# Two residual graph layers in Strassen form on one core: order of GpSimd's, VectorE's and ScalarE's side work

## The chip, the cores and the metric

The kernel runs on one core of a Trainium2 chip. The metric is the device time of one execution in microseconds (us), the median of several executions. Engines are named as in the profile: PE is TensorE's matmul, PEld its weight load, DVE is VectorE, ACT is ScalarE, POOL is GpSimd, and SP issues the DMAs.

## The reference

There are 64 graphs of 256 nodes with 512 features, in float32. Two layers run one after the other, each with a residual and a layer norm:

```
# layer 0
deg = sum(adj, -1);  agg = (adj @ x) / max(deg, 1e-6)
x1  = layernorm(x + relu(concat([x, agg]) @ W.T))
# layer 1
q, k, v = x1 @ Wqk (two halves), x1 @ Wv
w   = sum(q * (adj @ (k * mask)), -1) * mask / sqrt(512)
out = layernorm(x1 + softmax(w over the nodes) * v)
```

The softmax runs over the 256 nodes of a graph, so each node ends with one weight for its row of v. Layer norm takes mean and variance over the 512 features.

## The kernel before

**Tiling.** The graphs go in 32 pairs (`for j in range(NP)`). Every product of layer 0 is done once with W's two halves (W0), and in layer 1 with Wv and with Wq times Wk transposed (W1), which the kernel works out at its start. Each product is in Strassen form with seven products instead of eight, P1 to P7, of sums of blocks: S1 to S4 are sums of the left side, T1 to T4 of the right side. Some of the seven are split once more in the same form (`inner`). The sums of the left sides, X for layer 0 and Y for layer 1, live in a `Side`: xT_s and x1T_s in the profile, their inner sums in xT_i and x1T_i. S4 has no room of its own: in xT_s it is written over S1, in x1T_s over S2.

**Units.** A product is a list of units, each of one to three matmuls and the copies and additions that belong to it. `run("i k i k", ...)` pops units by letter, and this is TensorE's order, written out by hand. In layer 0: i is P1, k is P5, m is P2, p is P6 (left side S2), q is P7 (S3), r is P3 (left side S4), s is P4. P1 and P2 use the same bank, `pw[0]`. `inner` has four units; its third unit fills a part of the output bank by a copy on ScalarE, and the fourth accumulates onto it. l is P3 of layer 1 (`open1`), spread over the start of the next pair.

**Gather.** The products with adj are units a to g (`gather`), also seven. For layer 0, `a` and `b` end with two additions each on VectorE into own (`onto`, scalar_tensor_tensor with 1/deg), out of banks u and p2; `d`, `e` and `g` accumulate onto u. The right side is the y of layer 0, whose sums T1 to T4 (`sums_T`, tile tv) are made on VectorE. `spare()` in a, b and d pops a sum that was kept for later (`later`, `T_late`).

**Side work.** The layer norms, the masks, the degrees, the softmax and the weight sums are chains of steps. `tick`, at the end of each unit, places steps while the engine's modelled time `eng.free` isn't over `room` (0.6) ahead of the modelled clock and the chain's `ready` time is reached; lines 131 to 133 hold the modelled costs. `flush(names)` places at once whatever is left of a chain. Since every engine works in the order of the program, a step that is placed early blocks what stands behind it:

```
ready[0] = eng.free + (0.4 if eng is not vec else 2.2 if name == "finish"
                       else 0.7 if len(steps) == NT else 1.4)
```

`norm_of` is the layer norm's chain: mean (`less`, VectorE), two squares with a sum (junk, ScalarE), factor (rstd, two small ScalarE operations), `shift` (VectorE), two scales (ScalarE). "norm" is the first layer's, "finish" the second's; finish's scales release the store of out. Behind that store, on the same queue, stands the load of the next adj, and its landing starts adj's four sums on GpSimd (sa). The masked adj has four such sums too.

**The last pair** has its own code behind the loop: softmax over a row in PSUM, `b3` adds P3 and its fifth inner product on VectorE, then for each half of the rows product, `bn_stats`, factor, scale and store.

Of the kernel before, what the change touches and what calls it, by code (L numbers as in the profile page):

```python
# [35 lines left out]
F32 = mybir.dt.float32  # L36
BF16 = mybir.dt.bfloat16
AF = mybir.ActivationFunctionType
OP = mybir.AluOpType
AX = mybir.AxisListType  # L40

P = 128
# [5 lines left out]
S1, S2, S3, S4 = range(4)  # L48
# [46 lines left out]
def resnorm_kernel(  # L95
# [46 lines left out]
    def step(chain):  # L142
        _, name, ready, steps = chain
        eng, work = steps.popleft()
        work()
        ready[0] = eng.free + (0.4 if eng is not vec else 2.2 if name == "finish" else 0.7 if len(steps) == NT else 1.4) if steps and steps[0][0] is not eng else 0.0
        if not steps:
            chains.remove(chain)

# [9 lines left out]
    def flush(*names):  # L159
        while True:  # L160
            c = next((c for c in chains if not names or c[1] in names), None)
            if not c:
                return
            step(c)

    def run(order, **units):
        for name in order.split():
            units[name].pop(0)()
# [7 lines left out]
    def first(out, in_):  # L176

        return tc.keep_in_program_order(nc.sync.dma_start(out, in_))
# [101 lines left out]
                (eng, lambda: eng.tensor_sub(a(S2), a(S1), a(A11))),  # L280
                (eng, lambda: eng.tensor_sub(a(S3), a(A11), a(A21)))]

    def fourth_sums(X):

        ks = slice(0, 2)
        gp.tensor_sub(X.block(S4, ks), X.block(A12, ks), X.block(S2, ks))
        inner_sums(X, gp, 2)

    def run_now(steps):
        for _, work in steps:  # L290
            work()

    def inner_sums(X, eng, part):

        if X.s is None:
            X.open_sums()
        of_sum = lambda n: lambda k, e: X.s[:, k, X.slot[n]:X.slot[n] + 1, e]
        ks, b = ((slice(0, 2), X.first_row), (slice(2, 3), of_sum(S1)), (slice(0, 1), of_sum(S4)))[part]
        a11, a12, a21, a22 = (b(k, e) for k in range(2) for e in range(2))
        i = [X.i[:, r, ks] for r in range(4)]  # L300
        for to, op, c, d in ((i[0], OP.add, a21, a22), (i[1], OP.subtract, i[0], a11),
                             (i[2], OP.subtract, a11, a21), (i[3], OP.subtract, a12, i[1])):
            eng.tensor_tensor(to, c, d, op=op)

    def adj_sums(j):
        a, s = adjs[j], pool.tile([P, 4, 2, P], F32, name="sa", bufs=2)
        a11, a21, a12, a22 = (a[:, :, t, h * P:(h + 1) * P] for t in range(2) for h in range(2))
        gp.tensor_add(s[:, 0], a21, a22)
        gp.tensor_sub(s[:, 1], s[:, 0], a11)
        gp.tensor_sub(s[:, 2], a11, a21)  # L310
        gp.tensor_sub(s[:, 3], a12, s[:, 1])
        return {"A11": a11, "A12": a12, "A22": a22, "S1": s[:, 0], "S2": s[:, 1], "S3": s[:, 2], "S4": s[:, 3]}
# [71 lines left out]
            return go  # L384
        return [unit(e) for e in range(H)]

    def sums_T(val, later=None):

        b11, b12, b21, b22 = (val[:, :, t, h * HF:(h + 1) * HF] for t in range(NT) for h in range(2))
        tv = pool.tile([P, 4, 2, HF], F32, name="tv")  # L390
        t1, t2, t3, t4 = (tv[:, r] for r in range(4))
        vec.tensor_sub(t1, b12, b11)
        rest = [lambda args=args: vec.tensor_sub(*args) for args in ((t2, b22, t1), (t3, b22, b12), (t4, b21, t2))]
        if later is None:
            for do in rest:
                do()
        else:
            later.extend(rest)
        return {"B11": b11, "B21": b21, "B22": b22, "T1": t1, "T2": t2, "T3": t3, "T4": t4}

    def gather(a, w, dst, u, p5, p2, own=None, rdeg=None, later=()):
# [69 lines left out]
        return dict(a=[u1], b=[g2], c=[g5], d=[u2], e=[u3], f=[g3], g=[u4])  # L471


    def norm_of(src, total):

        rstd, shift, less, var = (small.tile([P, NT], F32, name=x) for x in ("rstd", "shift", "less", "var"))

        def mean():
            vec.tensor_scalar(less, total, -1.0 / F, None, op0=OP.mult)

        def square(t):
            junk = small.tile([P, F], BF16, name="junk", bufs=1)
            act.activation(junk, src[:, t], AF.Square, bias=less[:, t:t + 1], accum_out=var[:, t:t + 1])

        def factor():
            act.activation(rstd, var, AF.Ln, bias=eps, scale=1.0 / F)
            act.activation(rstd, rstd, AF.Exp, scale=-0.5)

        def shifts():
            vec.tensor_tensor(shift, less, rstd, op=OP.mult)  # L490

        def scale(t):
            act.activation(src[:, t], src[:, t], AF.Identity, bias=shift[:, t:t + 1], scale=rstd[:, t:t + 1])
        return [(vec, mean)] + [(act, lambda t=t: square(t)) for t in range(NT)] + [(act, factor), (vec, shifts)] + [
            (act, lambda t=t: scale(t)) for t in range(NT)]

    def layer_norm(src, mv, n, by_vec):

# [255 lines left out]
    for j in range(NP):  # L754
# [17 lines left out]
        if j == 0:  # L772
            run("i k i k i k i k", i=i, k=k)
            flush("degrees")
            load_rows(1)
        elif j == 1:
            early.append(a1)
            run("k i k i k i k", i=early[0], k=k)
            fourth_sums(X)
            run("m p p m p p m", m=m, p=p)  # L780
            load_x(1)
        else:
            run("i k", i=i, k=k)
            send_scores(j - 2)
            run("i l k", i=i, k=k, l=open1)
            flush("norm")
            fetch_scores(j - 2)
            places[0](range(16))
            run("i k i k", i=i, k=k)
        if j != 1:  # L790
            fourth_sums(X)
        if j > 1:
            flush("mask")
            sumsM[j - 1] = adj_sums(j - 1)
# [4 lines left out]
            softmax(j - 2)  # L799
            shared[0] = 1.0  # L800
        if j != 1:
            run("m p p m p p m", m=m, p=p)
        flush("w0a")
        run("q q q", q=q)
        flush("w0")
        run("r q r m", m=m, q=q, r=r)
        if j == 1:
            flush("norm", "mask")
            sumsM[0] = adj_sums(0)
            load_rows(2)  # L810
        quiet[0] = j < 2
        room[vec] = -9.0 if j > 1 else 0.6
        run("r s r", r=r, s=s)
# [3 lines left out]
            inner_sums(Y, gp, 0)  # L817
            queue(1, "sums", *outer_sums(Y, vec), (vec, lambda Y=Y: inner_sums(Y, gp, 1)))
        T_late = []
        T = sums_T(ys[j], T_late if j < 2 else None)  # L820

        if j == 0:
            degrees(1)
# [11 lines left out]
        if j == 0:  # L835
            sums_next()
            held = [c for c in chains if c[1] == "w1"]
            chains[:] = [c for c in chains if c[1] != "w1"]
            early.append(inner("P1", Xs[1], W0, pw[0], u, lambda fifth: early[1](fifth)))
            run("s s a b s d c e i g f", s=s, i=early[0], **g)  # L840
            quiet[0] = False
        else:
            u2, o2, y2 = o, pf, y
            b1, b2, b3, b4, b5, b6, b7, b8 = layer1(j - 1, ys[j][:, :, 0], o2, u2, y2)
            jj = inner("P1", Y, W1, pw[0], u2)
            k = inner("P2", Y, W1, y[0], o2, b2)
            if j == 1:
                turn_here(Y, owns[0], 0, pw)
                run("s", s=s)
                turn_here(Y, owns[0], 1, pw)  # L850
                inner_sums(Y, gp, 0)
                sums_Y = (*outer_sums(Y, vec), (vec, lambda: inner_sums(Y, gp, 1)))
                run("s b a s d c", s=s, **g)
                quiet[0] = False
                flush("w1")
                run("e j g f", j=jj, **g)
                queue(1, "sums", *sums_Y)
                run("k j k j k j", j=jj, k=k)
                b1(None)
                run("k", k=k)  # L860
            else:
                run("s s j s a b", s=s, j=jj, k=k, **g)
                room[vec] = 0.6
                run("j", j=jj)
                if j < NP - 1:
                    degrees(j + 1)
                run("c d j k e j", s=s, j=jj, k=k, **g)
                quiet[0] = True
                run("k", k=k)
                quiet[0] = False  # L870
                b1(None)
                run("g f", **g)
# [78 lines left out]
    for _, turn, exps in last:  # L951
        turn()
        exps()
    run("r", r=r)
    flush()
    probs[j] = small.tile([P, 2, NT], F32, name="probs", bufs=2)
    for k in range(2):
        last[k][0](pw[k])
    b3(held[0])
    for k in range(2):  # L960
        vec.tensor_copy(probs[j][:, k], pw[k][:, :NT])
    norms = []

    def close(k, t, scale):
        for _, work in scale:
            work()
        first(out[2 * j + k, t * P:(t + 1) * P], x1[:, k, t])
    for t in (1, 0):
        for k in range(2):
            o = x1[:, k, t:t + 1]  # L970
            vec.scalar_tensor_tensor(o[:, 0], vs[j][k][:, t], probs[j][:, k, t:t + 1], o[:, 0],
                                     op0=OP.mult, op1=OP.add)
            stats, scale = layer_norm(o, small.tile([P, 1, 2], F32, name="mv"), 1, (t, k) == (0, 1))
            run_now(stats + scale[:1])
            norms.append((k, t, scale[1:]))
            if len(norms) == 2:
                close(*norms.pop(0))
    close(*norms.pop(0))


# [24 lines left out]
```

## Time and profile before

| | |
|---|---|
| median of 3 executions | 1886.93 us (1886.43 to 1887.25) |
| profiled span | 1884.5 us, granted TensorE clock 0.997 |
| from the last matmul's end to the end of the span | about 13 us |
| S4 over xT_s on GpSimd | one operation, 128x512, 1.27 us |
| stage of one pair | about 57 us |

A line of the timeline gives the start and the length in us, the engine, the line of the helper that issued it (all side work is L90, all products are L173), the operation, the tiles written and read, their shapes, and how many like operations are merged. In square brackets stands idle time before it and who ended it, as the semaphores suggest.

### The profile page before, as it was taken

To read this page: it belongs to the slowest core of one execution; us is meant where nothing else is said; L and a number is where in the kernel's file an instruction comes from. 1 tells how busy PE (TensorE), PEld (TensorE's weight loads), DVE (VectorE), ACT (ScalarE), POOL (GpSimd) and SP (SyncE) were. 2 spreads that over 40 slices of the span, in tenths; PEclk is the share of its full clock that TensorE was granted. 3 is DMA by queue.
4 is the path that set the end of the run, shared out by engine and by line. 5 is a ranking of instruction groups with operands and counts; after the bars stand their busy time and mean duration, and the time that the engine had idled before them with its cause. 6 is when DMAs were issued, how large, how long until landed. Compare 5 with 4: busy or idle time off the path is not lost.

```text
span 1884.5 us, 24896 instructions
## 1 busy us (share of the span) xinstructions
PE 1861.3 (99%) x6996; PEld 1312.9 (70%) x6996; DVE 1541.9 (82%) x3182; ACT 1303.6 (69%) x3270; POOL 896.5 (48%) x1187
## 2 busy tenths in 40 slices
PE   9999999999999999999999999999999999999997
PEld 5667767767777677677677677676776777776764
DVE  7787888788888878887888888788878888878887
ACT  3667776677776677766777776777676777667765
POOL 4455453555454554435554435454445544355532
PEclk9999999999999999999999999999999999999998
DMA  6133334333333333343433343333434233433321
GB/s 225 56 74 81 99 90 118 85 97 92 103 96 103 100 83 97 90 118 85 104 88 101 96 114 89 84 98 95 112 85 108 84 102 95 118 85 88 98 62 51
DMA packets 380713, 181.26 MB, mean 96 GB/s; under 512 B 263712, under 2 KB 345248, under 8 KB 380576
## 3 DMA queue, kind: packets, MB, share of 16 engines
q1 hardware_dynamic: 380576, 179.67, 35.5%
q8 instruction: 57, 0.93, 0.2%
q14 instruction: 80, 0.66, 0.1%
HBM read 114.10 MB, written 34.06 MB: 79 GB/s over the span
## 4 chain that ended last, share of the span: by engine, by line
PE 92%; DVE 5%; ACT 1%; POOL 1%; issue 1%; DMA 0%; DVEq 0%; ACTq 0%
PE bank L173 92%; DVE own L90 2%; DVE tv L90 1%; DVE y L90 1%; POOL xT_s L90 1%; ACT y L90 0%; ACT own L90 0%; DMA wqk<-wqk_t 0%; PE bank L625 0%; ACT bank L90 0%; DVE st L90 0%; DVE t L90 0%; DVE x L90 0%; DVE v L90 0%; ACT junk L90 0%
## 5 line engine op out<-in xcount | busy, mean ns | idle before, releaser
L90 ACT COPY bank<-bank 128x256 f32<-128x256 f32 (+1 forms) x768 | 332.6, 436 | 241.0 <-PE bank L173 231.9
L90 DVE TENSOR_TENSOR y<-bank,y 128x512 f32<-128x512 f32 x256 | 170.6, 687 | 133.2 <-ACT y L90 132.2
L90 ACT ACTIVATE junk<-own,less 128x512 bf16<-128x512 f32 x252 | 182.5, 724 | 64.8 <-DVE less L90 63.9
L90 ACT ACTIVATE own<-own,shift,rstd 128x512 f32<-128x512 f32 x255 | 200.4, 812 | 0.0
L173 PE MATMUL bank<-tv,sa 128*128 128x256 f32 x768 | 194.7, 381 | 4.0 <-DVE tv L90 1.8
L90 POOL TENSOR_TENSOR x1T_s<-x1T,x1T_s 128x512 f32<-128x512 f32 x32 | 53.2, 1663 | 280.9 <-PE bank L173 280.9
L173 PEld LDWEIGHTS bank<-tv,sa 128*128 128x128 f32 x768 | 144.8, 190 | 56.0 <-issue 22.9
L90 ACT COPY y<-bank 128x512 f32<-128x512 f32 x192 | 108.9, 584 | 94.9 <-PE bank L173 93.5
L90 POOL TENSOR_TENSOR sa<-adj 128x256 f32<-128x256 f32 x128 | 95.6, 747 | 159.3 <-DMA adj<-adj_t 150.5
L173 PE MATMUL bank<-w,x1T_s 128*128 128x512 f32 (+1 forms) x384 | 168.4, 521 | 0.0
L90 POOL TENSOR_TENSOR x1T_i<-x1T 128x256 f32<-128x256 f32 x64 | 55.6, 868 | 228.6 <-DMA x1T<-turn 213.3
L173 PE MATMUL bank<-t,xT_s 128*128 128x512 f32 (+1 forms) x384 | 160.2, 526 | 2.4 <-POOL xT_s L90 1.5
L90 POOL TENSOR_TENSOR x1T_i<-x1T_s 128x128 f32<-128x128 f32 x128 | 76.6, 598 | 177.4 <-DVE x1T_s L90 174.9
L90 DVE TENSOR_TENSOR v<-bank,v 128x512 f32<-128x512 f32 x186 | 119.2, 683 | 48.8 <-PE bank L173 48.8
L173 PE MATMUL bank<-t,x1T_s 128*128 128x512 f32 (+1 forms) x384 | 158.2, 522 | 0.3 <-ACT y L90 0.3
L173 PE MATMUL bank<-w,xT_s 128*128 128x512 f32 (+1 forms) x384 | 153.2, 521 | 0.0
L173 PE MATMUL bank<-t_i,xT_i 128*128 128x256 f32 x512 | 152.7, 380 | 0.4 <-POOL sa L90 0.2
L173 PE MATMUL bank<-t_i,x1T_i 128*128 128x256 f32 x512 | 152.3, 379 | 0.1
L173 PEld LDWEIGHTS bank<-t_i,x1T_i 128*128 128x128 f32 x512 | 97.2, 190 | 67.0 <-issue 49.7
L90 ACT COPY own<-bank 128x512 f32<-128x512 f32 x128 | 71.8, 587 | 93.5 <-PE bank L173 49.4
L173 PEld LDWEIGHTS bank<-t_i,xT_i 128*128 128x128 f32 x512 | 94.9, 190 | 58.1 <-issue 46.3
L173 PE MATMUL bank<-t,x1T 128*128 128x512 f32 x256 | 130.5, 593 | 0.0
(156 smaller groups left out, 4610.1 us busy)
## 6 DMA issues: line engine op xcount, KB each, us to landing
x<-x SPq DMA_DIRECT2D x64, 512.0 KB, 5.7
xT<-x_t SPq DMA_DIRECT2D x62, 512.0 KB, 5.5
out<-own SPq DMA_DIRECT2D x62, 512.0 KB, 3.2
x1T<-turn SPq DMA_DIRECT2D x480, 64.0 KB, 2.3
adj<-adj_t SPq DMA_DIRECT2D x64, 256.0 KB, 3.8
turn<-adj SPq DMA_DIRECT2D x64, 256.0 KB, 3.0
row<-d SPq DMA_DIRECT2D x31, 256.0 KB, 4.7
wqk<-wqk_t SPq DMA_DIRECT2D x4, 512.0 KB, 5.3
```

Source lines behind the costliest of these rows:

```text
L90: return self.tc.keep_in_program_order(getattr(self.engine, name)(out, *args, **kwargs))
L173: tc.keep_in_program_order(nc.tensor.matmul(ps, a, b, start=start, stop=True, skip_group_check=True))
```

## The change

Five edits, none of which changes what is computed.

- **S4 graph by graph**: `fourth_sums` writes S4 for graph 1 and for graph 0 in two operations. In layer 0 the second comes after the first two units of P6, and the inner sums after it.
- **Later sums of y**: of the four sums of y, two (from pair 2 on) are kept for `spare()` and so stand behind the additions of a and b.
- **norm's squares later**: the chain "norm" waits 2.2 instead of 1.4 of modelled time between the mean and the squares.
- **Last variances on ScalarE**: in the last pair the first two row halves take their variance from the sum and ScalarE's squares; P3's fifth product is added by matmuls with the identity; the additions of P3 are spread.
- **First pairs' orders mixed**: in pair 0 two more units change place; in pair 1 P2's first unit comes between P1 and P5, a is ahead of b, and the flush of the masks and the masked sums move behind the first transposes.

The diff, cut to its core:

```diff
-        ready[0] = ... (0.4 if eng is not vec else 2.2 if name == "finish" else 0.7 if len(steps) == NT else 1.4) ...
+        ready[0] = ... (0.4 if eng is not vec else 0.7 if name == "norm" and len(steps) == NT else 2.2 if name in ("finish", "norm") else 1.4) ...
...
-    def fourth_sums(X):
-        ks = slice(0, 2)
-        gp.tensor_sub(X.block(S4, ks), X.block(A12, ks), X.block(S2, ks))
-        inner_sums(X, gp, 2)
+    def fourth_sums(X, ks=(1, 0)):
+        for k in ks:
+            k = slice(k, k + 1)
+            gp.tensor_sub(X.block(S4, k), X.block(A12, k), X.block(S2, k))
+        if ks[-1] == 0:
+            inner_sums(X, gp, 2)
...
-    def sums_T(val, later=None):
+    def sums_T(val, later=None, n=3):
...
+        for do in rest[:n]:
+            do()
+        if n < len(rest):
+            later.extend(rest[n:])
...
-            run("k i k i k i k", i=early[0], k=k)
-            fourth_sums(X)
-            run("m p p m p p m", m=m, p=p)
+            run("k i k m k i k", i=early[0], k=k, m=m)
+            fourth_sums(X, [1])
+            run("p p", p=p)
+            fourth_sums(X, [0])
+            run("m p p m", m=m, p=p)
...
-            fourth_sums(X)
+            fourth_sums(X, [1])
...
-            run("m p p m p p m", m=m, p=p)
+            run("m p p", m=m, p=p)
+            fourth_sums(X, [0])
+            run("m p p m", m=m, p=p)
...
-            flush("norm", "mask")
-            sumsM[0] = adj_sums(0)
-            load_rows(2)
+            flush("norm")
...
-        T = sums_T(ys[j], T_late if j < 2 else None)
+        T = sums_T(ys[j], T_late, 0 if j < 2 else 1)
...
-            run("s s a b s d c e i g f", s=s, i=early[0], **g)
+            run("s s a b s c d i e i g f", s=s, i=early[0], **g)
...
                 turn_here(Y, owns[0], 0, pw)
+                flush("mask")
+                sumsM[0] = adj_sums(0)
+                load_rows(2)
...
-                run("s b a s d c", s=s, **g)
+                run("s a b s d c", s=s, **g)
...
     run("r", r=r)
+    for k in range(2):
+        mm(y[k][:, HF:], ident, held[0])
     flush()
...
-    b3(held[0])
+    add_p3(0)
...
-    for t in (1, 0):
-        for k in range(2):
-            o = x1[:, k, t:t + 1]
-            vec.scalar_tensor_tensor(o[:, 0], vs[j][k][:, t], probs[j][:, k, t:t + 1], o[:, 0],
-                                     op0=OP.mult, op1=OP.add)
-            stats, scale = layer_norm(o, small.tile([P, 1, 2], F32, name="mv"), 1, (t, k) == (0, 1))
-            run_now(stats + scale[:1])
-            norms.append((k, t, scale[1:]))
-            if len(norms) == 2:
-                close(*norms.pop(0))
-    close(*norms.pop(0))
+    for k in range(2):
+        total = small.tile([P, 1], F32, name="total2", bufs=2)
+        stt(k, 1, accum_out=total)
+        steps = norm_of(x1[:, k, 1:2], total, 1)
+        run_now(steps[:3])
+        norms.append((k, 1, steps[3:]))
+    add_p3(1)
+    for k in range(2):
+        stt(k, 0)
+        stats, scale = layer_norm(x1[:, k, 0:1], small.tile([P, 1, 2], F32, name="mv"), 1, k == 1)
+        run_now(stats)
+        close(*norms.pop(0))
+        run_now(scale[:1])
+        norms.append((k, 0, scale[1:]))
+    for norm in norms:
+        close(*norm)
```

More of the change, by code (lines that the diff above doesn't have):

```diff
@@ L145, in step @@
         work()
-        ready[0] = eng.free + (0.4 if eng is not vec else 2.2 if name == "finish" else 0.7 if len(steps) == NT else 1.4) if steps and steps[0][0] is not eng else 0.0
+        ready[0] = eng.free + (0.4 if eng is not vec else 0.7 if name == "norm" and len(steps) == NT else 2.2 if name in ("finish", "norm") else 1.4) if steps and steps[0][0] is not eng else 0.0
         if not steps:
@@ L393, in sums_T @@
         rest = [lambda args=args: vec.tensor_sub(*args) for args in ((t2, b22, t1), (t3, b22, b12), (t4, b21, t2))]
[L394 to L398, printed above, removed]
+        for do in rest[:n]:
+            do()
+        if n < len(rest):
+            later.extend(rest[n:])
         return {"B11": b11, "B21": b21, "B22": b22, "T1": t1, "T2": t2, "T3": t3, "T4": t4}
@@ L471, in gather, with norm_of @@
         return dict(a=[u1], b=[g2], c=[g5], d=[u2], e=[u3], f=[g3], g=[u4])
-    def norm_of(src, total):
-        rstd, shift, less, var = (small.tile([P, NT], F32, name=x) for x in ("rstd", "shift", "less", "var"))
+    def norm_of(src, total, n=NT):
+        rstd, shift, less, var = (small.tile([P, n], F32, name=x) for x in ("rstd", "shift", "less", "var"))
         def mean():
@@ L493, in scale @@
             act.activation(src[:, t], src[:, t], AF.Identity, bias=shift[:, t:t + 1], scale=rstd[:, t:t + 1])
-        return [(vec, mean)] + [(act, lambda t=t: square(t)) for t in range(NT)] + [(act, factor), (vec, shifts)] + [
-            (act, lambda t=t: scale(t)) for t in range(NT)]
+        return [(vec, mean)] + [(act, lambda t=t: square(t)) for t in range(n)] + [(act, factor), (vec, shifts)] + [
+            (act, lambda t=t: scale(t)) for t in range(n)]
     def layer_norm(src, mv, n, by_vec):
@@ L958, in resnorm_kernel, with add_p3, stt, close @@
         last[k][0](pw[k])
-    b3(held[0])
+    def add_p3(k):
+        vec.tensor_add(vs[j][k][:, 0], y[k], vs[j][k][:, 0])
+    def stt(k, t, **more):
+        vec.scalar_tensor_tensor(x1[:, k, t], vs[j][k][:, t], probs[j][:, k, t:t + 1], x1[:, k, t],
+                                 op0=OP.mult, op1=OP.add, **more)
+    def close(k, t, scale):
+        run_now(scale)
+        first(out[2 * j + k, t * P:(t + 1) * P], x1[:, k, t])
+    add_p3(0)
     for k in range(2):
@@ L962, in resnorm_kernel @@
     norms = []
[L964 to L967, printed above, removed]
-    for t in (1, 0):
-        for k in range(2):
-            o = x1[:, k, t:t + 1]
-            vec.scalar_tensor_tensor(o[:, 0], vs[j][k][:, t], probs[j][:, k, t:t + 1], o[:, 0],
-                                     op0=OP.mult, op1=OP.add)
-            stats, scale = layer_norm(o, small.tile([P, 1, 2], F32, name="mv"), 1, (t, k) == (0, 1))
-            run_now(stats + scale[:1])
-            norms.append((k, t, scale[1:]))
-            if len(norms) == 2:
-                close(*norms.pop(0))
-    close(*norms.pop(0))
+    for k in range(2):
[14 more added lines that the diff above has]
+        close(*norm)
 def kernel(x, adj, nodemask, L0_gnn_W, L1_gnn_Wqk, L1_gnn_Wv):
```

## The prediction

> **What bounds the kernel now.** I read the busy times first, then the starts of successive matmuls (how much later than the plain spacing of 0.43 us for 512 columns and 0.215 for 256 does each begin?), then the timeline round the late ones.
>
> ```profile
> PE 1861.3 (99%) x6996; PEld 1312.9 (70%) x6996; DVE 1541.9 (82%) x3182; ACT 1303.6 (69%) x3270; POOL 896.5 (48%) x1187
> ```
>
> TensorE is the bound, at a granted clock of 0.997; the change removes no matmul and adds two. So it can only move late starts and the two ends. Late starts of over 60 ns sum to 28.6 us: 9.7 before 95 us (pairs 0 and 1), 16.6 in the steady pairs, 2.4 after 1835 us; behind them lies a tail of 13.5 us. The steady 16.6 are three kinds: 7.2 us where unit p starts (22 pairs; 5.5 of waiting and 0.075 each for the restart), 3.4 us in nine pairs where gather's d follows c, and 5.9 us at P5's third unit, which the change leaves alone.
>
> Gather's d, pair 22:
>
> ```profile
> 1285.60 1.26 DVE L90 TENSOR_TENSOR y<-y,fifth 128x512 f32<-128x512 f32 x1
> 1286.89 1.10 DVE L90 TENSOR_TENSOR tv<-y 128x512 f32<-128x512 f32 x1
> 1288.02 0.69 DVE L90 TENSOR_TENSOR tv<-y,tv 128x512 f32<-128x512 f32 x1
> 1288.63 0.68 DVE L90 TENSOR_TENSOR tv<-y 128x512 f32<-128x512 f32 x1
> 1289.23 0.68 DVE L90 TENSOR_TENSOR tv<-y,tv 128x512 f32<-128x512 f32 x1
> 1289.60 2.29 PE L173 MATMUL bank<-tv,sa 128*128 128x256 f32 x8
> 1289.83 1.65 DVE L90 SCALAR_TENSOR_TENSOR own<-bank,rdeg,own 128x256 f32<-128x256 f32 x4
> ```
>
> The eight tv,sa matmuls are c and d; four should take 0.86 us, but d begins at 1290.76, 0.30 late. It writes bank u, which the first two of the four additions must read first; those stand behind four sums T1 to T4 of y.
>
> Unit p, pair 18:
>
> ```profile
> 1036.42 0.72 POOL L90 TENSOR_TENSOR sa<-adj,sa 128x256 f32<-128x256 f32 x1
> ...
> 1036.62 0.81 DVE L90 TENSOR_TENSOR v<-v,fifth 128x256 f32<-128x256 f32 x1
> ...
> 1038.40 1.30 DVE L90 STREAM_TRANSPOSE turn<-own 128x512 f32<-128x512 f32 x2
> 1039.52 1.27 POOL L90 TENSOR_TENSOR xT_s<-xT,xT_s 128x512 f32<-128x512 f32 x1 [2.37 <-PE bank L173]
> 1039.62 1.39 DVE L90 TENSOR_TENSOR bank<-bank,fifth 128x256 f32<-128x256 f32 x4
> ...
> 1040.06 1.07 ACT L90 COPY own<-bank 128x512 f32<-128x512 f32 x2 [1.45 <-DVE bank L90]
> ...
> 1040.79 1.96 PE L173 MATMUL bank<-t,xT_s 128*128 128x512 f32 x4
> ```
>
> The list of waits names POOL's S4 (xT_s, ending 1040.79). That is not the releaser: in pairs with no stall p starts 0.22 us before S4 ends, and in every late pair it starts 0.14 us after ScalarE's first copy of own ends. That copy waits for VectorE, which lost time at v<-v,fifth: 0.43 alone, 0.81 here, beside GpSimd's last sa operation.
>
> [...]v<-v,fifth (both inputs in SBUF) takes 0.43 to 1.01 us, while bank<-bank,fifth beside S4 keeps its 0.40. [...]I count sa by its starts, 0.69 to 0.80 apart.
>
> **Part by part.**
>
> *Later sums of y (n=1).* T1 and T2 stay ahead, T3 and T4 move behind the additions of a and b. The additions then follow T2: 1288.63 instead of 1289.83, 1.2 us earlier, and d is 0.3 late. The next user of T3 is e, behind c, d, j and k, over 3 us on; T4 is needed by g. Gone: nine late starts of 0.19 to 0.30 and their restarts of 0.105, **-3.4 us**. At pairs 0 and 1 all three sums were already deferred.
>
> *S4 by graph.* Two half operations (0.73 each, as the 256-element sa) for one of 1.27. In steady pairs GpSimd now does S4 of graph 1, the four masked sa (2.9 us), then S4 of graph 0 and four inner sums (2.6 with the first): it starts 1.05 us before p and ends 5.1 us after it; P3, the first reader, comes 7.3 us after p. Nothing waits, and the wait it seems aimed at is ScalarE's: **0**.
>
> *norm's squares later (2.2 for 1.4).* In steady pairs ScalarE stood idle 1.51 us for `less` (to 1133.62, in pair 19). Following `step` and `tick` with their own costs: graph 0's squares come one and three units later, graph 1's factor falls behind gather's copy of g, and the two last finish scales run behind both. From g's copy at 1142.05: 0.47 + 0.42 + 0.72 + 0.82 ends them at 1144.48 instead of 1144.26, **0.2 us** later. They release the store of out, and the load of adj is queued behind that store; its landing starts the four sa beside v<-v,fifth. Set against when p is due, the first sa begins 6.38 to 6.11 us before it in 18 late pairs (0.17 to 0.44 late, rising one for one), 6.08 to 5.86 before in eight on-time pairs (9.56 in pair 2), and 5.81, 5.76 and 5.34 before in three that are 0.06, 0.11 and 0.34 late: a sawtooth[...]. Shifting all of them by 0.2 us and reading the sawtooth again leaves 5.4 of the 7.2 us, **-1.8 us**; by 0.3 it leaves 3.9, by 0.5 it makes 7.9. Next behind the finish scales is P3's first copy (due 1144.59): 0.1 us of room.
>
> *First pairs.* Pair 0: c before d, and P1's second unit moved up to the wait of g: 0.43 us of work inside stalls, -0.4. Pair 1: m's first unit uses the bank of P1 (pw[0]) and waits for i's last copies, +0.4. More: by the same bookkeeping norm's last residual now stands ahead of P1's fifth additions on VectorE, which went at 58.17; they go at 58.9, own is copied at 59.4, and p starts near 60.1 instead of 59.36: +0.75 with all before it. Then the flush of norm:
>
> ```profile
> 69.89 0.15 DVE L90 TENSOR_TENSOR shift<-less,rstd 128x2 f32<-128x2 f32 x1
> ...
> 70.62 1.28 DVE L90 TENSOR_TENSOR own<-bank,own 128x512 f32<-128x512 f32 x2
> 70.66 1.51 ACT L90 ACTIVATE own<-own,shift,rstd 128x512 f32<-128x512 f32 x2
> ...
> 72.07 0.58 ACT L90 COPY bank<-bank 128x512 f32<-128x512 f32 x1
> ...
> 72.70 0.70 PE L173 MATMUL bank<-t_i,xT_s 128*128 128x256 f32 x2 [0.67 <-ACT bank L90]
> ```
>
> Now the shift precedes P2's additions to own (1.28, then 0.98 with fifth). With the factor one unit later, the shift isn't ready when P2 ends and is flushed behind them: additions from about 71.3, shift near 73.4, two scales 1.5, P3's copy 0.57, P3's last unit near 75.7 instead of 72.70: +3.0, the 0.75 included, although the wait before P3's third unit (0.4) goes. Afterwards a ahead of b lets d wait less (1.3 before; now some 0.3 at a and 0.3 to 0.5 at d): -0.5. Together **+2.5 us** (1.0 to 3.3). The masks' flush finds nothing left, so the masked sums moved behind it cost nothing.
>
> *The end.* Fifth is added by two identity matmuls (0.86 us) instead of two DVE additions (0.34 of spacing each); one of P3's two additions moves behind the first products; two bn_stats and bn_aggr (0.81 a graph) become squares on ScalarE, which waits there anyway. Before, the first product began at 1872.90. Now: PE ends 1869.99 + 0.86 = 1870.85, the eight small matmuls 1.05, copies to 1872.15. Then VectorE: two times 0.81 (product, mean), addition 0.62, two times 1.65 (product 0.79, stats 0.73, the rest): ready at 1877.7. ScalarE: scale 0.72, factor 0.5, last shift 0.2 and scale 0.55: about 1879.9, against 1880.82: **-0.9 us** (0.5 to 1.2). The store after it is the same.
>
> Sum: -3.4 - 1.8 + 2.5 - 0.9 = -3.6: 1886.9 - 3.6 = **1883.3**.
>
> **Rivals.** (A) The sum above, 1883.3. (B) The adj loads shift 0.3 us, where most sawtooth waits vanish (-3.3), and the second pair costs only 1.0, because VectorE's backlog is shorter than I carried over: -3.4 - 3.3 - 0.9 + 1.0 = -6.6, 1880.3. For it: 18 of 29 pairs lie just before the quiet stretch. Against: g's copy fixes the shift near 0.2. (C) The loads stay or go 0.4 later (no gain, waits of 0.2 to 0.4 in most pairs) and the second pair costs 3.3: -3.4 - 0.9 + 3.3 = -1.0, 1885.9. For it: the waits depend on landings that vary by 0.5 us. (D) Slower: the finish scales slip further, P3's first copy is late, and its second unit stalls 0.3 + 0.075 us in 29 pairs: +10.9 - 3.4 - 0.9 + 2.5 = +9.1, 1896.0. For it: 0.1 us of room at the copy and 0.17 in the bank. Against: the chain from g's copy is counted from steps that the trace times.
>
> **How the numbers follow.** A 0.40, B 0.33, C 0.20, D 0.07. The bound for faster is 1886.93 less 0.2%, 1883.2; A lies on it and counts 0.19 to faster, 0.21 to same. Faster 0.19 + 0.33 = 0.52; same 0.21 + 0.20 = 0.41; slower 0.07. The range takes in B with another 1.3 us[...] (1879.0) and C with 0.9 for the early pairs (1886.8), and leaves out D.
>
> **What would show it.** Right: no late d in steady pairs; `less` idle of ScalarE down from 1.5 us; p still late in part of the pairs, by other amounts, always 0.14 us after ScalarE's copy; P3's last unit of pair 1 over 2 us later than 72.70; the span ending about 11.7 us after the last small matmul (13.2 before). Wrong: p never late (then S4 or the loads were worth 7 us), new late starts at P3's second unit, or pair 1 finishing as early as before.

## The result, and the profile after

The changed kernel takes 1885.65 us (median of 4 runs, 1884.56 to 1886.5) against 1887.09 (4 runs, 1886.43 to 1887.43) for the kernel before, beside it on the chip: ratio 0.9992, 95% interval 0.9975 to 1.001. That is -1.4 us and can't be told from no change. The forecast, 1883.3, was 2.4 us too low. The profiled spans are 1884.5 before and 1883.9 after.

The busy line of the page, and from the list of waits of TensorE its three largest (in total, times, longest, us), both of the changed kernel:

```profile
PE 1860.9 (99%) x7000; PEld 1314.8 (70%) x7000; DVE 1511.7 (80%) x3180; ACT 1309.5 (70%) x3274; POOL 909.7 (48%) x1251
```

```profile
PE bank L173 <- ACT bank L90: 4.4, 3, 3.6
PE bank L173 <- POOL sa L90: 1.9, 8, 0.3
PE bank L173 <- ACT own L90: 1.3, 1, 1.3
```

TensorE is still the bound. New is one wait of 3.6 us for ScalarE. I measured all stages in one way: a late start is the start of a matmul less the start of the one before, less the plain spacing. Places in the first pairs are measured from the first xT_i product, which itself begins at a different time in every run:

| us | before | after | difference |
|---|---|---|---|
| first xT_i product of pair 0, from the span's start | 20.14 | 21.44 | +1.30 |
| p of pair 1, from that product | 39.21 | 39.96 | +0.75 |
| first transposes of pair 1 | 53.53 | 57.01 | +3.48 |
| first x1T_s product of pair 1 | 72.37 | 76.69 | +4.32 |
| late starts of p, steady pairs | 7.18 | 5.36 | -1.83 |
| late starts of d, steady pairs | 3.46 | 0.00 | -3.46 |
| last softmax's transposes to the last operation | 12.19 | 11.22 | -0.97 |

The first and the last four rows add up to -0.64; the two spans differ by -0.61. So these places account for the whole difference between the two traces. Each column is one execution, though, and the start and the waits of p differ from one execution to the next.

**The cost: pair 1.** The timeline where P3's last unit (t_i,xT_s into bank) is due, changed kernel:

```profile
72.71 1.28 DVE L90 TENSOR_TENSOR own<-bank,own 128x512 f32<-128x512 f32 x2
...
74.03 0.70 DVE L90 TENSOR_TENSOR own<-own,fifth 128x512 f32<-128x512 f32 x1
74.65 0.67 DVE L90 TENSOR_TENSOR shift<-less,rstd 128x2 f32<-128x2 f32 x1
...
75.36 1.52 ACT L90 ACTIVATE own<-own,shift,rstd 128x512 f32<-128x512 f32 x2 [2.83 <-DVE shift L90]
...
76.78 0.57 ACT L90 COPY bank<-bank 128x512 f32<-128x512 f32 x1
...
77.41 0.70 PE L173 MATMUL bank<-t_i,xT_s 128*128 128x256 f32 x2 [3.63 <-ACT bank L90]
...
78.45 1.91 PE L626 MATMUL bank<-ident,own 128*128 128x128 f32 x8
...
80.16 1.80 PE L173 MATMUL bank<-t,agg 128*128 128x512 f32 x2
...
81.79 1.04 PE L626 MATMUL bank<-ident,own 128*128 128x128 f32 x8
```

Read it upward from the matmul at 77.41. It waited 3.63 us for a copy of ScalarE; the copy stood behind two scales, the scales waited 2.83 us for the shift, and the shift stood behind VectorE's additions. Before, the shift came ahead of the additions, at 69.89. Now look at the lengths below it: eight transposes took 1.91 us at 78.45 and 1.04 at 81.79, and the two t,agg matmuls 1.80, where before they took 1.02. The windows view of the same trace says why. After the stretch and its length stand the busy times of PE, PEld, DVE, ACT and POOL with their instructions, then the granted clock of TensorE, the DMA share and GB/s:

```profile
60.00:77.00 17.00, 12.52 (x39) 7.05 (x38) 13.40 (x29) 12.97 (x31) 6.87 (x10) 1.00 0.46 155
77.00:82.00 5.00, 4.59 (x16) 3.29 (x17) 2.67 (x4) 1.84 (x5) 0.00 (x0) 0.66 0.00 0
```

Asked in shorter stretches, the same view gives a clock of 1.00 from 77.41 to 78.30, 0.50 from 78.30 to 81.70 and 1.00 behind that. So TensorE ran at half speed for 3.4 us (transposes 0.213 us apart, not 0.109), which costs half of that, 1.7 us. The drop came 0.9 us after work had begun again (77.41 to 78.30).

**The gain: d.** Pair 22 again, changed kernel:

```profile
1288.61 0.69 DVE L90 TENSOR_TENSOR tv<-y,tv 128x512 f32<-128x512 f32 x1
1289.22 0.87 DVE L90 SCALAR_TENSOR_TENSOR own<-bank,rdeg,own 128x256 f32<-128x256 f32 x2
...
1290.01 0.68 DVE L90 TENSOR_TENSOR tv<-y 128x512 f32<-128x512 f32 x1
1290.20 1.89 PE L173 MATMUL bank<-tv,sa 128*128 128x256 f32 x8
1290.60 0.87 DVE L90 SCALAR_TENSOR_TENSOR own<-bank,rdeg,own 128x256 f32<-128x256 f32 x2
1291.39 0.68 DVE L90 TENSOR_TENSOR tv<-y,tv 128x512 f32<-128x512 f32 x1
```

The additions of a stand straight behind T2, T3 and T4 follow them, and the eight matmuls of c and d run through in 1.89 us (2.29 before).

**Half a gain: p.** One of the pairs still late, changed kernel:

```profile
1553.85 0.73 POOL L90 TENSOR_TENSOR sa<-adj,sa 128x256 f32<-128x256 f32 x1
1553.86 1.00 DVE L90 TENSOR_TENSOR v<-v,fifth 128x256 f32<-128x256 f32 x1
...
1556.76 0.73 POOL L90 TENSOR_TENSOR xT_s<-xT,xT_s 128x256 f32<-128x256 f32 x1 [2.18 <-PE bank L173]
1557.06 1.39 DVE L90 TENSOR_TENSOR bank<-bank,fifth 128x256 f32<-128x256 f32 x4
...
1557.49 1.07 ACT L90 COPY own<-bank 128x512 f32<-128x512 f32 x2 [1.64 <-DVE bank L90]
...
1558.22 1.96 PE L173 MATMUL bank<-t,xT_s 128*128 128x512 f32 x4 [0.25 <-POOL sa L90]
```

S4 of graph 1 (xT_s) now ends at 1557.49, 0.7 us ahead of p, and p is late all the same; "POOL sa" in the bracket can't be the releaser either, since p reads no sa. The chain is the one of before: sa beside v<-v,fifth (1.00 instead of 0.43), the additions, ScalarE's first copy of own, and p 0.14 us after that copy. Late by over 60 ns are now 15 pairs instead of 20. (The 22 pairs of the prediction are those whose second matmul shows the restart; of these there are now 17.)

**The end.** The last softmax's transposes begin at 1868.63 before and at 1868.99 after, so I count from them. The first product begins 3.48 us behind them (forecast: 1872.15, that is 3.52; before: 4.27), and the last operation ends 11.22 us behind them (forecast: 1879.9, that is 11.3; before: 12.19).

### The profile page after: what moved, and what is told of

Its sections match the earlier page's. It is cut to its first block, busy times and chain, and to the rows that moved or that the text cites. A ratio compares the mean times of both kernels' runs of the same rounds, so it can differ in the third digit from the quotient of the medians.

```text
span 1883.9 us, 25002 instructions
## 1 busy us (share of the span) xinstructions
PE 1860.9 (99%) x7000; PEld 1314.8 (70%) x7000; DVE 1511.7 (80%) x3180; ACT 1309.5 (70%) x3274; POOL 909.7 (48%) x1251
## 4 chain that ended last, share of the span: by engine, by line
PE 96%; POOL 1%; issue 1%; DVE 1%; ACT 0%; DMA 0%; DVEq 0%; POOLq 0%; ACTq 0%
PE bank L173 96%; POOL xT_s L90 1%; POOL xT_i L90 0%; DVE own L90 0%; POOL sa L90 0%; DMA wqk<-wqk_t 0%; PE bank L626 0%; ACT own L90 0%; ACT bank L90 0%; DVE st L90 0%; ACT y L90 0%; PE bank L649 0%; DVE tv L90 0%; DVE shift L90 0%; DVE bank L90 0%
## 5 line engine op out<-in xcount | busy, mean ns | idle before, releaser
L90 POOL TENSOR_TENSOR x1T_s<-x1T,x1T_s 128x256 f32<-128x256 f32 x64 | 63.7, 1014 | 267.4 <-PE bank L173 267.4
L90 POOL TENSOR_TENSOR x1T_i<-x1T_s 128x128 f32<-128x128 f32 x128 | 101.1, 790 | 182.8 <-DVE x1T_s L90 182.8
```

Source lines behind the costliest of these rows:

```text
L90: return self.tc.keep_in_program_order(getattr(self.engine, name)(out, *args, **kwargs))
```

## The experiments

**One edit at a time on the kernel before: later sums.**

```diff
+T = sums_T(ys[j], T_late, 0 if j < 2 else 1)     # and sums_T with n
```

> Kernel before with the later sums of y alone. If d's late starts come from T3 and T4 standing ahead of the additions on VectorE: no late d in the steady pairs (3.4 us less), the wait of p as before (7 us in all), pairs 0 and 1 as before: about 1883.6 us. Rival, the additions were late for another reason[...]: d's late starts stay near 0.3 in some nine pairs and the time stays near 1887.

Measured: 1883.38 us against 1886.53, ratio 0.9983 (0.9975 to 0.9990). Late starts of d: none; late starts of p 7.16 us, as before. The term of -3.4 stands: the edit by itself takes 3.2 us off the time.

**S4 graph by graph alone.**

```diff
-fourth_sums(X); run("m p p m p p m", m=m, p=p)
+fourth_sums(X, [1]); run("m p p", m=m, p=p); fourth_sums(X, [0]); run("m p p m", m=m, p=p)
```

> Kernel before with S4 by graph alone (pairs 0 and 2 to 31, and layer 1; pair 1 keeps its order). If p waits for ScalarE's copy of own: p's late starts stay between 6 and 8 us in all, and always 0.14 us after that copy ends; time within 1 us of before. Rival, the list of waits is right and p waits for S4: p's late starts vanish, 7 us less, about 1880.

Measured: 1885.57, ratio 0.9997 (0.9990 to 1.0004): no change that can be told. S4's half is done well ahead of p, and p is still late by 5.50 us in 16 pairs, 0.14 us after ScalarE's copy each time. So the wait that the list puts down to S4 isn't S4's. But 5.50 is less than the 6 to 8 that I expected. The edit moved the phase: in every steady pair the store of out is issued 11.33 us before p is due, instead of 11.10, and adj's sums begin 0.1 to 0.2 us earlier. How much of the 1.7 us comes of that is open: the profiled execution was the fastest of the 20 (1883.27), and in it d's late starts too were fewer than before.

**The later squares alone.**

```diff
-... 2.2 if name == "finish" else 0.7 if len(steps) == NT else 1.4
+... 0.7 if name == "norm" and len(steps) == NT else 2.2 if name in ("finish", "norm") else 1.4
```

> Kernel before with the 2.2 for norm alone. If the rule moves the finish scales and with them the store of out and the load of adj: the store is issued 10.9 instead of 11.1 us before p is due, the first sa comes 0.2 us later, and p's late starts fall from 7.2 to about 5.4 us. In pair 1, with the old orders, shift falls behind P2's additions to own: P3's last unit is at least 2 us later than before and TensorE's clock drops behind the wait. Sum: about 2 us slower, 1889. Rival, the mixed orders and not the rule cost the time in pair 1: pair 1 stays as before and the time falls by 1.8 to 1885.3.

Measured: 1889.36, ratio 1.0013 (1.0004 to 1.0021), +2.8 us. The wait ahead of P3's last unit is 3.63 us, as in the changed kernel, the granted clock behind it 0.66 over 77 to 82 us, and the first x1T_s product comes 76.80 us after the first xT_i product (72.37 before). The store moves to 10.90 before p is due, 0.2 later, and p's late starts are 6.04 us (5.4 expected). One line does both: a small gain at p and the whole cost in pair 1.

**The new end alone.**

```diff
+for k in range(2): mm(y[k][:, HF:], ident, held[0])   # and the new order of the last products, squares for bn_stats
```

> Kernel before with the end alone. From the start of the last softmax's transposes to the last VectorE operation 0.9 to 1.0 us less, nothing else moves: about 1886.1 us. Rival, the identity matmuls delay the small matmuls as much as the removed additions gave: 0.2 us or less.

Measured: 1886.54, ratio 0.9997 (0.9988 to 1.0006). The end is 11.21 us long instead of 12.19, as expected, but with p's late starts at 7.69 and a later start of the first product (21.22) nothing of it is seen in the time. 1 us is below what these runs tell apart. The four edits alone come to -3.2 - 1.0 + 2.8 + 0.0 = -1.4, as much as all five together; but each of these times is uncertain by over 1 us and the mixed orders aren't among them, so the agreement proves little.

**Are the mixed orders or the squares to blame?** The changed kernel with the first pairs' old orders:

```diff
-run("k i k m k i k", ...); fourth_sums(X, [1]); run("p p"); fourth_sums(X, [0]); run("m p p m")
+run("k i k i k i k", ...); fourth_sums(X); run("m p p m p p m")     # and c, i, a, b, the masks' flush as before
```

> The changed kernel with the first two pairs' orders of before (P2's first unit behind P1, c behind d, b before a, the masks' flush in its old place, S4 of pair 1 in one operation), but norm's later squares kept everywhere. Theory: the rule alone, with no help of the mixed orders, throws the shift of pair 0's norm behind P2's additions. So unit p of pair 1 is back where it was before (39.2 us after the first xT_i product, 39.96 in the changed kernel), but the wait ahead of P3's last unit stays at 3 to 4 us, the transposes behind it run at half speed, and the first x1T_s product comes 76.3 to 77.3 us after the start (72.4 before, 76.7 changed). Time within 1 us of the changed kernel's. Rival: the mixed orders push VectorE's queue back; then the wait falls to about 0.7 us and the time is about 3.5 us less than the changed kernel's.

Measured: 1885.21, ratio 0.9991 (0.9985 to 0.9998). p of pair 1 is back at 39.21, but the wait is 3.63 us again, the clock 0.66 again, and the first x1T_s product comes at 76.79. The mixed orders cost p 0.75 us and gain as much later (a before b). The squares are to blame. (The ratio, here and below, is to the kernel before. A time can be set against the changed kernel's only through that one's -1.4 us, whose interval reaches from -4.7 to +1.9, so the places in the traces are the sharper measure.)

**The old allowance for pair 0's norm alone.**

```diff
-... 2.2 if name in ("finish", "norm") else 1.4
+... 2.2 if name == "finish" else lag[0] if name == "norm" else 1.4     # lag[0] = 1.4 for pair 0, then 2.2
```

> The changed kernel, with the allowance of 1.4 kept for the norm of pair 0 alone and 2.2 from pair 1 on. Theory: the shift is ready before P2 ends and goes ahead of P2's additions; the wait ahead of P3's last unit of pair 1 falls from 3.63 to about 1 us, TensorE keeps its clock, and the first transposes of pair 1 come some 54.0 us after the first xT_i product instead of 57.0. With a before b kept, the first x1T_s product comes at 72.0 to 72.6 instead of 76.7. Time 4 to 4.5 us below the changed kernel, that is about 5.5 below the kernel before. Rival (the mixed orders cause the wait): 76.7 and the changed kernel's time stay.

Measured: 1880.72 against 1887.04, ratio 0.9966 (0.9955 to 0.9978), 6.3 us below the kernel before (5.5 expected). The timeline, with the shift ahead of the additions again:

```profile
71.70 0.15 DVE L90 TENSOR_TENSOR shift<-less,rstd 128x2 f32<-128x2 f32 x1
...
72.44 1.28 DVE L90 TENSOR_TENSOR own<-bank,own 128x512 f32<-128x512 f32 x2
...
74.52 0.70 PE L174 MATMUL bank<-t_i,xT_s 128*128 128x256 f32 x2 [0.67 <-ACT bank L90]
75.05 0.59 PE L174 MATMUL bank<-w,xT_i 128*128 128x256 f32 x2
75.48 1.04 PE L628 MATMUL bank<-ident,own 128*128 128x128 f32 x8
```

The wait is 0.67 us, the transposes take 1.04 at once, the granted clock over 77 to 82 us is 1.00 instead of 0.66, and the first x1T_s product comes at 72.33 instead of 76.69. The wait and the half clock go together.

**Is it the idleness that halves the clock?** The changed kernel with the wait filled by products that nothing reads:

```diff
+if j == 1:
+    for _ in range(4): matmul(pw[0], w0[:, 0, :P], w0[:, 0])    # ahead of P3's last unit
```

> The changed kernel, with four products of 128x512 added in pair 1 ahead of P3's last unit, whose results nothing uses; each is two matmuls of 0.43 us, 3.4 us in all, inside the wait of 3.63 us. Theory: the half speed behind the wait (transposes 0.215 us apart instead of 0.109 until about 81.8 us) comes of TensorE standing idle. Filled, the transposes run at 0.109, the granted clock of the 5 us from P3's last unit on is 0.95 or more instead of 0.66, and the first x1T_s product comes 1.4 to 1.8 us earlier (about 75.0 us after the first xT_i product instead of 76.7). Rival: the clock falls there for another reason (the load up to then, a fixed time after the start): the slow stretch stays, or moves, and nothing is gained.

Measured: 1884.18, ratio 0.9982 (0.9975 to 0.9989). Timeline, and below it the window of the same 5 us:

```profile
73.77 3.60 PE L819 MATMUL bank<-w 128*128 128x512 f32 x8
77.58 0.70 PE L173 MATMUL bank<-t_i,xT_s 128*128 128x256 f32 x2 [0.21 <-ACT bank L90]
78.11 0.59 PE L173 MATMUL bank<-w,xT_i 128*128 128x256 f32 x2
78.55 1.04 PE L626 MATMUL bank<-ident,own 128*128 128x128 f32 x8
```

```profile
77.00:82.00 5.00, 4.79 (x25) 3.09 (x24) 2.67 (x4) 3.42 (x8) 0.37 (x1) 1.00 0.00 0
```

P3's last unit comes no earlier (77.58), yet the transposes take 1.04 us and the first x1T_s product comes at 75.01, 1.68 us sooner. Work without any use made this stage faster, and with it the granted clock of the same 5 us is 1.00 instead of 0.66: the half clock came of the idle time. The times agree (2.9 us below the kernel before, where the changed kernel is 1.4 below it), but they alone wouldn't show it.

**Does the load of adj set p?** In the traces of the two kernels every v<-v,fifth of over 0.45 us, 28 before and 23 after, lies beside an sa (so do 2 and 7 of the shorter ones); why it takes longer there they don't show. The changed kernel with the load of adj, which adj's sums wait for, ahead of the store of out:

```diff
-run("a n b q d q n c q e q n p g f", ...); b8()        # then, in the next pair: load_adj(j)
+run("a n b q d q n c q e q n p g", ...); load_adj(j + 1); run("f", **g); b8()
```

> The changed kernel, with the load of the next pair's adj issued behind gather's g, ahead of the store of out in the same queue, in every pair but the last. Theory: [...]Freed from the store, adj lands about 2.5 to 3.5 us earlier, the sums start 8.5 to 9.6 us before p is due, and are done before v<-v,fifth: the waits of p in the steady pairs fall from 5.4 us to under 1, and the time falls by 4.5 to 5.4 us. Rival: p is late for VectorE's own backlog, or the sums meet other operations of VectorE instead: the waits stay above 4 us, the time within 1.5 us of the changed kernel's.

Measured: 1880.27, ratio 0.9962 (0.9948 to 0.9976). The same pair as the last one above:

```profile
1544.05 0.72 POOL L90 TENSOR_TENSOR sa<-adj 128x256 f32<-128x256 f32 x1 [1.34 <-DMA adj<-adj_t]
...
1549.85 0.42 DVE L90 TENSOR_TENSOR v<-v,fifth 128x256 f32<-128x256 f32 x1
...
1552.91 1.07 ACT L90 COPY own<-bank 128x512 f32<-128x512 f32 x2 [1.07 <-DVE bank L90]
...
1553.80 1.88 PE L173 MATMUL bank<-t,xT_s 128*128 128x512 f32 x4
```

Adj's sums start 9.74 us before p, are done before v<-v,fifth (0.42, its plain length), and p follows with no wait in its bracket. In no steady pair does a v<-v,fifth now take over 0.45 us, where in the changed kernel 23 of 60 did, up to 1.01, and before 28 of 60. p's late starts fall from 5.36 to 0.27 us. The runs also draw together: 5 runs within 0.6 us, where the three other variants of the changed kernel so far scatter over 3.7 to 5.6 us (6 to 20 runs).

**All of it.** The changed kernel with the last allowance, the earlier load, and P2's first unit of pair 1 behind P1 and P5 again:

```diff
-run("k i k m k i k", i=early[0], k=k, m=m); fourth_sums(X, [1]); run("p p", p=p)
+run("k i k k i k", i=early[0], k=k); fourth_sums(X, [1]); run("m p p", m=m, p=p)     # with the last but two and the last edit
```

> The changed kernel with the allowance of 1.4 kept for pair 0's norm, adj loaded ahead of the store of out, and P2's first unit of pair 1 back behind P1 and P5 (the other mixed orders stay). Theory: the gains lie at different places and add up: against the changed kernel 4.4 us at P3's last unit and the clock behind it, 5.1 to 5.4 at p of the steady pairs, 0.75 at p of pair 1: some 10.3 in all, so about 11.5 us below the kernel before, ratio near 0.994, p of pair 1 at 39.2 us after the first xT_i product, the first x1T_s product 71.5 to 72.4 us after it, waits of p under 1 us. Rival: with P2's first unit later, the shift of pair 0's norm misses the end of P2 again or adj meets another operation, and one of the gains is lost: 6 to 7 us below the kernel before.

Measured: 1875.1 (1874.33 to 1875.4) against 1886.26, ratio 0.9935 (0.9922 to 0.9949): 11.2 us less than before, faster than both kernels. p of pair 1 comes at 38.96, the first x1T_s product at 71.25, p's late starts are 0.27 us. The list of waits of TensorE begins:

```profile
PE bank L174 <- ACT bank L90: 2.1, 5, 0.7
PE bank L174 <- DVE ones L90: 1.2, 1, 1.2
```

No wait of over 1.2 us is left, and the gains add up.

## Why the prediction came out as it did

The time lies in the range given, 1879.0 to 1886.8, but the forecast itself was 2.4 us off, and its chances leaned the wrong way: 0.52 for faster and 0.41 for the same, and it was the same. Step by step:

- **Later sums, -3.4: right.** -3.46 in the trace, -3.2 in the run with this edit alone.
- **S4 graph by graph, 0: right in what it denied.** S4 never released p. By itself the edit does shift the store of out by 0.23 us earlier, which I hadn't seen; with the later squares beside it the store stands at 10.90, as with the squares alone.
- **Squares later, -1.8: right in path; that the size fits is partly chance.** The store moved 0.2 us, p's late starts fell by 1.83. That the landing of adj sets them is shown by the earlier load, with which they fall from 5.36 to 0.27 us. But the squares alone took only 1.1 us off p in their trace, and S4 alone 1.7. In the five traces with the later squares everywhere or from pair 1 on, and adj behind the store, the late starts are 5.36, 6.04, 5.88, 4.78 and 4.69, in the three with neither these nor the split S4 7.18, 7.16 and 7.69. So something between 1 and 3 us is gained, and how it divides between the two edits stays open. What the edit took off ScalarE's own waits is no measure of it: those for `less` fell from 63.9 to 2.1 us over the span, and at most some 2 us of it reached TensorE.
- **First pairs, +2.5: the mis-sized term; it measured +4.3.** The path was right: p +0.75 (forecast 0.75), the shift behind P2's additions, P3's last unit +3.41 (forecast +3.0), a before b -0.77 (forecast -0.5; with the old allowance for pair 0 the first transposes still come 0.74 us later than before and the first x1T_s product 0.04 earlier). What was left out is the price of a wait so long: 1.7 us of half clock behind it. I had worked out a stop of about 3.7 us there (0.67 before, and 3.0 more) and added it as if a wait cost only its length. The four traces with the wait show the half clock there (0.66 over 77 to 82 us in each); in the kernel before, with the old allowance for pair 0, with the wait filled and with all of it together the clock of that stretch is 1.00.
- **The end, -0.9: right**, -0.97. (The prediction's terms as listed end at 1879.7, 0.2 us before the 1879.9 that it wrote; the trace, shifted to the same transposes, ends at 1879.85.)

With +4.3 in the sum it reads -3.4 - 1.8 + 4.3 - 0.9 = -1.8, 1885.1; measured were 1885.65. The rest lies within the scatter, to which the start adds: the first xT_i product began between 20.1 and 22.0 us in the eleven profiles. What sets that start I didn't try. Of the rivals the third, 1885.9, came closest, but for half a wrong reason: it let the gain at p fail, which didn't fail.

## What to carry to other kernels

In this kernel a stop of TensorE of 3.63 us cost its own length and 1.7 us more; where such a stop can't be removed, filling it with useless matmuls may win that back: here it won 1.68 us. A rule that delays a side chain in every stage must be looked at in the first stages by themselves, where the queues stand differently: here it gained 1 to 2 us over 30 pairs and lost over 4 in one. And where a wait comes and goes from stage to stage with the landing of a load, don't trim the operation the list names; move the load: here p's late starts fell from 5.36 to 0.27 us with it.

## What the runs showed that I hadn't expected

- In the four traces with the long wait the half clock sets in after the work has begun again, and lasts 3.4 us in each: idle to 77.41 and slow from 78.3 to 81.7 in the changed kernel, to 76.63 and 77.8 to 81.2 with the squares alone, to 76.36 and 77.8 to 81.2 with the old orders, to 77.16 and 77.7 to 81.1 with the earlier load. Idle were 3.63 us in the profile's matmul times each time. The longest wait of the kernel before, 1.76 us ahead of the matmul at 46.83, left the clock at 1.00; lengths between weren't tried.
- With p's waits gone the scatter of the runs fell from about 5 us (the kernel before, 39 runs) to 0.6 and 1.1 (5 runs each). This suggests that most of what looked like noise of the measurement was one wait in the kernel; the waits themselves were counted in one execution of each kernel only.
